# Layer 0's attention: the query side of a tile in three turns, each beside other tiles' steps

## The chip, the cores and the metric

The kernel runs on one core of one Trainium2 chip. The metric is the device time of one launch in microseconds, the median of three runs. A core has an engine for matrix products (TensorE, PE in the profile, which writes its results to eight PSUM banks), two for elementwise work that can read PSUM (VectorE, DVE; ScalarE, ACT), a third for elementwise work and indirect transfers (GpSimd, POOL), and SyncE (SP), which issues most transfers.

## The reference

Four layers work on 1250 nodes with 512 features. Each adds a graph layer and a mixer to x, then a mixture of experts. The mixer of layer 0 is a small network of two blocks, each an attention and a perceptron. Its attention is linear, with 8 heads of 64 features and 256 random features per head:

```python
y = layernorm(x, ln1_g[i], ln1_b[i])
q, k, v = ...                                     # y @ Wq + bq and so on, split into heads
qp = softmax_kernel(q, proj[i], True)             # ratio * (exp(dash - diag - max) + 1e-4), 256 per head
kp = softmax_kernel(k, proj[i], False)
d_inv = 1.0 / einsum('bhnm,bhm->bhn', qp, kp.sum(axis=2))
ctx = einsum('bhnm,bhnd->bhmd', kp, v)
o = einsum('bhmd,bhnm,bhn->bhnd', ctx, qp, d_inv)
x = x + o @ Wo[i] + bo[i]
```

The rest of the program (experts, graph layers, the other mixers) is not touched by the change.

## The kernel before

Nodes are worked on in 10 tiles of 125 and in three chunks of 500, 500 and 250 (`CH`). Everything is float32 where this text goes; a float32 product is two PE instructions in the profile, so that four calls show as x8, while a transpose is one.

`l0_attention` (L843) runs twice, for the two blocks. Its first half makes keys and values and from them `cx`, the context: for each head and each half of the 256 features a 128 x 65 block, whose 65th column is the sum of the keys' features. Its second half, which is what changes, goes over the queries:

- Per chunk, four `proj_T` products give `qT`, the transposed queries, and ScalarE squares them into `sq` (L1049). Both have one buffer.
- `features_q` (L991) makes a tile's features. PE forms half the sum of squares per head (`halves,sq`, one bank) and the products with the random directions (`pj,qT`, four banks); DVE takes the maxima of each bank (L1004) and forms the negative bias `nb` (L1008, L1009); ACT takes the exponentials of the four banks into `qf` (L1012), one head at a time.
- `mixed` (L1015) does the rest of a tile. PE turns `qf` so that features lie on partitions, 16 transposes into four banks (L1020), each emptied by DVE with the addition of 1e-4 and the ratio into `qfT` (L1022). Then come the products with `cx`, four heads to a bank; DVE takes the reciprocal of the 65th columns and multiplies (L1033, L1034) into `ov`. PE turns `ov` (four transposes, L184, one bank), and `copy` empties that bank into `oT`: it takes DVE (L141) and ACT (L143) by turns, over the whole program. At last `oT` times `wo` (`w,oT` in the profile) is added by DVE to the residual (L261).

`mixed` runs one tile behind `features_q`: in each turn of the loop the features of tile t come first, then everything that is left of tile t-1. `aside`, called once a turn, adds edges to the graph in the first block and does nothing in the second.

Which engine an instruction runs on is written in the text. In what order an engine gets its instructions is set by a planner in the tile layer: it goes by the order of the text, and takes a later instruction where an earlier one isn't ready by its own costs. So the statistics of the next layer norm (`BATCH_NORM_STATS`, L191), which the text has behind the attention, stand in DVE's order within it, one after each tile's addition. PSUM banks come from one pool of eight (`bank`, L145). [...]

After the attention, `l0_mlp` normalises all tiles, turns them, and goes through the perceptron in four parts, whose weights use the same three buffers as `wq` and `wo`.

## Time and profile before

| what | value |
|---|---|
| median of 3 runs | 3299.57 us (3297.28 to 3302.95) |
| the profiled execution's own time | 3299.46 us |
| its span, first to last instruction | 3297.7 us |
| mean granted TensorE clock | 0.945 |
| query half, first block | 228 to 420 us: PE busy 172.4 of 193.0 us in 228 to 421 |
| query half, second block | 889 to 1080 us: PE busy 170.8 of 191.0 us |
| DVE, ACT busy in 228 to 421 | 87.8, 41.0 us |

A row of the profile names a line of the kernel, the engine, the operation, and what it writes and reads (out<-in, buffer numbers left out). Busy time counts an engine's own instructions; an idle time stands with the instruction that ended it, and with what that one had waited for. PEclk is the clock that PE was granted, as a share of full speed. Where a product comes from the helper `mm`, its line is L178 whatever calls it, so products are told apart by their tiles.

### The profile page before, as it was taken

The page shows a single profiled execution, that of the slowest core. Times are in us where ns is not written, and L with a number is a line of the kernel's source. Part 1 is how long each engine was busy: PE and PEld are TensorE (multiplying, and loading weights), DVE is VectorE, ACT ScalarE, POOL GpSimd, SP SyncE. Part 2 cuts the span into 40 slices and gives each one's busy share as a digit, 9 for nine tenths or more (in the row PEclk, how much of TensorE's full clock was granted, in tenths as well). Part 3 has the DMA queues.
Part 4 walks back from the last instruction along what each step waited for, and adds up shares of the span by engine and source line. Part 5 has one row for each costly group of instructions (what it writes and reads, how often), then busy time and mean ns, then how long its engine had stood idle before and what let it go on. Part 6 is the DMA issues. An engine that isn't in the chain of part 4 may idle for free. (4 is left out here: it accounts for less than half of the span.)

```text
span 3297.7 us, 31736 instructions
## 1 busy us (share of the span) xinstructions
PE 2947.0 (89%) x11563; PEld 1729.9 (52%) x11563; DVE 1185.3 (36%) x2903; ACT 731.9 (22%) x1511; POOL 677.7 (21%) x497
## 2 busy tenths in 40 slices
PE   7998889989988899989799987999799988779884
PEld 4556645455566454555455445766454547445552
DVE  6834431043344421243541352001334144352433
ACT  2222121122222212122230341221141013320121
POOL 4444444440000210013400011000301002022023
PEclk9999999999899899999899997999899999989987
DMA  7411112110000221217510016776310016530186
GB/s 220 108 14 1 16 17 46 33 30 14 13 1 14 59 69 39 57 37 218 172 47 1 7 32 222 244 241 208 99 39 1 1 53 197 177 103 1 32 291 196
DMA packets 236801, 277.58 MB, mean 84 GB/s; under 512 B 104719, under 2 KB 132735, under 8 KB 236625
## 3 DMA queue, kind: packets, MB, share of 16 engines
q1 hardware_dynamic: 126977, 189.85, 18.0%
q0 software_dynamic: 95968, 60.53, 8.2%
q10 hardware_dynamic: 13680, 24.91, 2.0%
q8 instruction: 104, 1.70, 0.2%
q14 instruction: 72, 0.59, 0.1%
HBM read 229.62 MB, written 45.17 MB: 83 GB/s over the span
## 5 line engine op out<-in xcount | busy, mean ns | idle before, releaser
L178 PE MATMUL ps<-xnT,w 128*128 128x500 f32 (+1 forms) x1584 | 571.9, 517 | 4.4 <-PEq L761 2.3
L178 PE MATMUL ps<-w,hT 128*125 128x512 f32 (+1 forms) x1232 | 540.4, 592 | 0.6 <-ACT hT L1199 0.6
L178 PEld LDWEIGHTS ps<-xnT,w 128*128 128x128 f32 x1584 | 299.9, 191 | 265.9 <-issue 251.2
L683 POOL DMA_INDIRECT adj<-count,cell x160 | 320.4, 2002 | 362.1 <-DMA adj<-count,cell 337.7
L178 PEld LDWEIGHTS ps<-w,hT 128*125 128x125 f32 (+1 forms) x1232 | 230.0, 189 | 276.8 <-issue 270.4
L178 PE MATMUL ps<-w,xnT 128*125 128x512 f32 x560 | 251.3, 598 | 0.0
L178 PE MATMUL ps<-xgT,w 128*128 128x256 f32 (+1 forms) x1256 | 235.3, 346 | 2.5 <-DVE xgT L510 1.7
L261 DVE TENSOR_TENSOR xn<-ps,xn 125x512 f32<-125x512 f32 x100 | 69.0, 691 | 455.2 <-PE ps L178 455.2
L178 PEld LDWEIGHTS ps<-xgT,w 128*128 128x128 f32 x1256 | 208.3, 194 | 43.7 <-issue 20.1
L468 POOL DMA_INDIRECT xg<-rows,r_idx x95 | 90.4, 952 | 627.6 <-PE ps L509 313.5
L587 ACT ACTIVATE hT<-ps,cols 128x500 f32<-128x500 f32 (+1 forms) x108 | 65.7, 608 | 553.1 <-PE ps L178 553.1
L178 PEld LDWEIGHTS ps<-w,xnT 128*125 128x125 f32 x560 | 103.6, 190 | 119.6 <-issue 118.4
L529 POOL DMA_INDIRECT came<-yd,slots x80 | 98.8, 1235 | 315.9 <-SPq L498 249.9
L510 DVE COPY xgT<-ps 128x512 f32<-128x512 f32 x95 | 62.6, 688 | 251.5 <-PE ps L509 233.9
L178 PE MATMUL ps<-hs,AT 125*125 125x512 bf16 x600 | 131.4, 379 | 3.8 <-PEq L761 3.8
L178 PE MATMUL ps<-AT,n 125*128 125x500 bf16 (+1 forms) x720 | 127.2, 339 | 0.0
L519 DVE TENSOR_TENSOR y<-ps,erow 128x512 f32<-128x512 f32 x71 | 49.1, 692 | 196.1 <-PE ps L178 184.1
L520 ACT ACTIVATE y<-y,r_w 128x512 f32<-128x512 f32 x71 | 51.2, 722 | 273.1 <-DVE y L519 254.6
L178 PEld LDWEIGHTS <-AT 125*125 125x125 bf16 x600 | 81.7, 136 | 55.5 <-issue 9.6
L178 PE MATMUL ps<-w,oT 128*125 128x512 f32 x160 | 92.1, 730 | 15.6 <-ACT oT L143 7.1
L184 PE MATMUL ps<-ident,z 125*128 125x125 f32 x320 | 61.1, 340 | 44.9 <-DVE z L199 25.3
L178 PEld LDWEIGHTS <-n 125*128 125x128 bf16 x720 | 69.9, 97 | 58.1 <-issue 1.1
(414 smaller groups left out, 3683.8 us busy)
## 6 DMA issues: line engine op xcount, KB each, us to landing
w<-in_L_ffn_we_dram SPq DMA_DIRECT2D x56, 1024.0 KB
w<-in_L_ffn_w_dram SPq DMA_DIRECT2D x60, 512.0 KB
yd<-y ACTq DMA_DIRECT2D x95, 256.0 KB
w<-in_L_mix_W_dram SPq DMA_DIRECT2D x16, 1024.0 KB
w<-in_L_ffn_w_dram SPq DMA_DIRECT2D x45, 256.0 KB
rows<-z SPq DMA_DIRECT2D x40, 224.0 KB
keyrow<-keys SPq DMA_DIRECT2D x16, 546.9 KB
erow<-in_L_ffn_b_dram SPq DMA_DIRECT2D x30, 256.0 KB
```

The lines of the kernel that those rows point to most:

```text
L178: nc.tensor.matmul(o, l, r, start=(i == 0), stop=(i == n - 1))
L184: nc.tensor.transpose(ps[:, tok(c)], src[:, fea(c)], ident[:TP, :TP])
L261: nc.vector.tensor_tensor(dst, ps, dst, op=OP.add)
L468: nc.gpsimd.indirect_dma_start(g, None, self.rows, bass.IndirectOffsetOnAxis(ap=self.idx[:, t:t + 1], axis=0))
L510: nc.vector.tensor_copy(xgT[:, :, j * SL:(j + 1) * SL], ps.rearrange("p (c s) -> p c s", c=NC))
L519: nc.vector.tensor_tensor(y, ps, bias, op=OP.add)
L520: nc.scalar.mul(y, y, scale)
L529: nc.gpsimd.indirect_dma_start(y, None, yd, bass.IndirectOffsetOnAxis(ap=slots[n][:, k * NT + t:k * NT + t + 1], axis=0))
L587: nc.scalar.activation(hT[:, f, :cn], ps[:, :cn], act, bias=b1(f))
L683: nc.gpsimd.indirect_dma_start(adj, bass.IndirectOffsetOnAxis(ap=self.cell[:, c:c + 1], axis=0), self.count[:, c:c + 1], None, compute_op= ...
```

## The change

`mixed` is cut in four: `turned_q` makes `qfT`, `attended` makes `ov`, `turned_out` makes `oT`, and `project` adds the product with `wo`. A turn of the loop now turns the features of tile t-1, makes the features of tile t, forms the products of tile t-1 with the context, projects tile t-2, and turns the output of tile t-1. The last two tiles are finished behind the loop. `oT` is always copied by ACT.

```diff
-            def mixed(t, qf):
+            def turned_q(qf):
                 qfT = qp.tile([P, H, 2, TP], F32, tag="qfT", name="qfT", bufs=2)
...
+                return qfT
+
+            def attended(qfT):
                 ov = qp.tile([TP, H, C], F32, tag="ov", name="ov")
...
+                return ov
+
+            def turned_out(ov):
                 oT = qp.tile([P, NC, TP], F32, tag="oT", name="oT", bufs=2)
-                copy(oT, transposed(ov.rearrange("p h c -> p (h c)")))
+                nc.scalar.copy(oT, transposed(ov.rearrange("p h c -> p (h c)")))
+                return oT
+
+            def project(t, oT):
                 ps = bank()
                 mm(ps[:TP, :], [(oT[:, c, :], wo[:, c, :]) for c in range(NC)])
                 add_to(xm[:, t, :], ps[:TP, :])
...
-            before = None
+            before, last = None, None
...
                 for t, o in tiles_of(c0, cn):
+                    if before is not None:
+                        qfT = turned_q(before[1])
                     qf = features_q(qT, sq, slice(o, o + TP))
                     if before is not None:
-                        mixed(*before)
+                        ov = attended(qfT)
+                        if last is not None:
+                            project(*last)
+                        last = before[0], turned_out(ov)
                     aside()
                     before = t, qf
-            mixed(*before)
+            qfT = turned_q(before[1])
+            project(*last)
+            oT = turned_out(attended(qfT))
+            project(before[0], oT)
```

## The prediction

> **What bounds the kernel now.** I read the page's first part, then the waits of TensorE (PE) in the two stretches that the change touches, then PE's timeline tile by tile, then the clock.

> The page says that PE is the bound, 2947 of 3297.7 us:

> ```profile
> PE 2947.0 (89%) x11563; PEld 1729.9 (52%) x11563; DVE 1185.3 (36%) x2903; ACT 731.9 (22%) x1511; POOL 677.7 (21%) x497
> ```

> The query half of layer 0's attention runs twice, from 228 to 420 us and from 889.5 to 1079.6 us. Who PE waits for in 228 to 421 (in total us, times, longest):

> ```profile
> PE ps L1020 <- DVE qfT L1022: 5.8, 8, 0.8
> PE ps L184 <- DVE ov L1034: 5.2, 10, 0.5
> PE ps L178 <- ACT oT L143: 3.5, 5, 0.7
> PE ps L178 <- DVE oT L141: 3.5, 4, 0.9
> ```

> Three waits per tile, each for the engine that empties PE's last product. PE's timeline shows what they cost (start, length, work, count, idle before):

> ```profile
> 273.53 3.70 PE L178 MATMUL ps<-w,oT 128*125 128x512 f32 x8 [0.67 <-ACT oT L143]
> 277.07 0.93 PE L178 MATMUL ps<-halves,sq 128*125 128x2 f32 x8
> 277.93 2.10 PE L178 MATMUL ps<-pj,qT 64*125 64x256 f32 x16
> 279.95 1.50 PE L1020 MATMUL ps<-ident,qf 125*128 125x125 f32 x12
> 282.28 0.65 PE L1020 MATMUL ps<-ident,qf 125*128 125x125 f32 x4 [0.83 <-DVE qfT L1022]
> 282.77 3.61 PE L178 MATMUL ps<-cx,qfT 128*125 128x65 f32 x32
> 286.21 0.38 PE L184 MATMUL ps<-ident,ov 125*128 125x125 f32 x2
> 287.11 0.43 PE L184 MATMUL ps<-ident,ov 125*128 125x125 f32 x2 [0.52 <-DVE ov L1034]
> 288.40 5.37 PE L178 MATMUL ps<-w,oT 128*125 128x512 f32 x8 [0.86 <-DVE oT L141]
> 293.61 13.58 PE L178 MATMUL ps<-xnT,w 128*128 128x500 f32 x32
> ...
> 409.16 1.87 PE L1020 MATMUL ps<-ident,qf 125*128 125x125 f32 x16
> 410.87 3.61 PE L178 MATMUL ps<-cx,qfT 128*125 128x65 f32 x32
> ```

> I count from start to start, since lengths contain the drain of the last product. Without waits: features F 277.07 to 279.95, 2.88 us; turning the features T (16 transposes, the row at 409.16) 1.71; products with the context A 3.44; turning the output O, 4 such transposes, 0.43; projection R 273.53 to 277.07, 3.54. Sum 12.00 us. The tile from 262.40 to 277.07 (projection to projection) took 14.67. So a tile loses 2.67 us, more than the 2.2 us of listed waits, because at each wait the pipeline drains too.

> The projection at 288.40 takes 5.37 us, the one at 273.53 3.70: same work. The windows say why (us; PE busy, instructions; granted clock):

> ```profile
> 254.40:257.80 3.40, 2.07 (x14) 1.00 0.13 1
> 257.80:261.20 3.40, 3.40 (x6) 0.50 0.12 1
> ...
> 264.60:268.00 3.40, 2.57 (x23) 1.00 0.09 5
> 268.00:271.40 3.40, 3.40 (x34) 1.00 0.05 0
> 264.60:268.00 3.40, 1.89 (x16) 1.00 0.09 5
> ```

> After a window of 3.4 us in which PE was busy 2.07 us, the next one ran at half clock. The last row counts the transposes alone. Cut into such windows, stretch one holds six half-clock windows (at 257.8, 288.5, 332.9, 350.0, 387.5, 404.6), each after one with 60 to 64% busy, and stretch two five (933.7, 978.0, 995.1, 1025.8, 1063.4). Each costs 5.37 - 3.70 = 1.67 us.

> **The change part by part.** PSUM banks come from a ring of 8 in text order, and in this trace PE takes the steps in text order even while it waits, so I take the new text as PE's new order: T(t-1), F(t), A(t-1), R(t-2), O(t-1).

> No arithmetic is added or taken away: the same matmuls, evictions, exponentials, no DMA, no queue passed over. What moves is what lies between a product and its reader:

> 1. T to A: the four evictions of qfT take 2.42 us on DVE (one group in the trace). They now have F's 2.88 us beside them. From T's start (0), the first bank is full at about 0.5, the last eviction ends by 3.0, and A begins at 1.71 + 2.88 = 4.6. Margin 1.6 us; 0.9 if one BATCH_NORM_STATS (0.69), which the planner puts into DVE's pauses here, stands ahead. The wait goes.
> 2. A to O: reciprocal and division (0.18 + 0.42 us) have R of an older tile, 3.54 us, beside them. The wait goes.
> 3. O to R: the copy of oT (0.57 on ACT) has a whole turn beside it. The wait goes. All copies are now ACT's: five more per stretch, 0.58 us each, in an engine that does 3.6 of 12 us; DVE loses five of 0.68. Without that cover it would be the present 0.7 us.
> 4. New wait: T(t) follows F(t) by A + R + O = 7.4 us; today another F and all of the previous tile lie between. Behind F come the last reduction (0.7), nb twice (0.3) and eight exponentials (3.02): done at about 4.6 + 4.1 = 8.7 on the tile's clock, T(t) at 12.0. Margin 3.3 us; behind that T all of PE would queue. Only in the first tile, which has no A, R, O before its T, does it bite: F(0) ends at 244.6, reductions at 246.0, exponentials from 246.4 to 249.5, T(0) ends at 250.0, F(1) at 252.9; A(0) begins at 252.9 instead of 251.6, 1.3 us late. O(0) has no R ahead and waits about 0.9 as now.
> 5. Banks: T and F together ask for 9 of 8; the ninth needs the first bank of T, emptied at about 1.2, and is asked for at 4.1. Free.
> 6. DVE: 2.6 + 2.5 + 0.8 + 0.7 + 0.7 + 0.4 + 0.6 = 8.3 us per tile (its groups from 262.40 to 277.07), of 12.0. It isn't the bound. What aside adds for the graph DVE has done by 152 us (L677), before stretch one.

> Sum, stretch one: O(0) ends and T(1) begins at about 257.7. Eight turns of 12.00 = 96.0; the projections of q for chunks two and three, 13.4 + 6.75; hence 373.9. Tail: T 1.71, R 3.54, A 3.44, O with both its waits 2.06, R 3.70 = 14.45. End 388.3, today 420.07: 31.8 us less. Stretch two has the same offsets (A(0) at 912.99, now 914.3); 135.4 us later it ends at 1049.7 instead of 1079.63: 29.9 less. Together 61.7; of this 11 x 1.67 = 18.4 is clock and 43.3 order.

> **The clock rule.** In the trace, full windows are followed by full clock. [...] No gap here is over 0.93 us and the clock falls all the same, so the row decides: part of a window idle is enough. [...] The new order puts O and T side by side, 2.14 us of transposes, then 0.86 us of tiny products; if they counted as idle, the clock would fall in many turns. The window at 264.6 was such a one: 1.89 us of transposes, 0.68 of other work, the rest idle, and the clock stayed at 1.00. The window at 254.4 had 0.81 of transposes, 1.26 of other work, and fell. So I count transposes as busy and take the clock as won, except for one window per stretch at the slow first tile or at the tail: 2 x 1.7 = 3.4 us given back.

> 61.7 - 3.4 = 58.3. The profiled execution took 3299.46 us (span 3297.7 and 1.8 around it), 0.1 below the median: **3241 us**.

> Nothing downstream holds this back: the only chain that runs by its own time, POOL's indirect additions to adj, ends at 749 us, and its first reader starts at 1080, about 1020 after the change. The weights for the perceptron are asked for when wq and wo come free (376.35 and 420.10), which move along.

> **The rivals.**
> - Clock not won. For: [...] outcomes near 60 to 65% busy go both ways (at 363.6, 60% busy, it didn't fall). Against: the window at 264.6. 3299.5 - 43.3 = 3256.
> - Half of the waits stay, because the planner orders DVE otherwise than the text: about 3270. For: today it sets nb between the evictions of qfT, where the text has it ahead of them. Against: T's banks are now full before F's.
> - Slower: DVE's order keeps the four reductions of F(t), nb and a BATCH_NORM_STATS ahead of the evictions of qfT. Then the last reduction ends at 5.4, and the evictions end at 5.4 + 0.3 + 0.7 + 2.4 = 8.8 instead of 3.0; A waits 4.2 us. It decides from 2.67 + 18.4/20 = 3.6 us per tile on. Here: (4.2 - 2.67) x 18 turns = +28, and a half-clock window in each turn instead of every other, + 0.75 x 18 = 13: 3340. Against: the bank ring lets F's ninth bank in only after an eviction, so at most part of it can happen.
> - It doesn't do what it says: the planner returns to the old order on PE, 3299. Against: PE has kept to the text in all 20 tiles.

> **How the numbers follow.** Likeliest 0.75 (3241, own range 3233 to 3250: two runs of before lie 5.7 us apart[...]); clock not won 0.12; half 0.06; slower 0.04; no effect 0.03. The range 3232 to 3262 takes in the first two. A change of 0.2%, 6.6 us, is about what a measurement tells from none: faster 0.93, same 0.03, slower 0.04.

> **What would show it.** PE's waits in the two stretches fall from 19.7 us each to about 5; all but the last projection of each stretch take about 3.7; the stretches last about 160 us; PE busy falls by the clock's 15 to 18 us. Wrong would be: rows of PE waiting for qf at L1012 in every turn (point 4), for qfT before A (point 1), or windows of 0.50 after windows full of transposes.

## The result and the profile after

The changed kernel takes 3261.98 us (median of 4, 3259.36 to 3276.86) beside 3301.26 for the kernel before: a ratio of 0.9887, 95% interval 0.9861 to 0.9913. Run again later it took 3260.24 us, ratio 0.9878 (0.9859 to 0.9897). It is faster, by 1.1 to 1.2% where 1.8% was forecast. 3299.57 x 0.9887 is 3262.3, at the upper edge of the range and just outside.

PE's row on the page after:

```profile
PE 2941.7 (90%) x11563; PEld 1740.8 (53%) x11563; DVE 1183.8 (36%) x2893; ACT 737.5 (23%) x1521; POOL 678.6 (21%) x497
```

PE's waits in the first stretch (in total us, times, longest), 228 to 395 us:

```profile
PE ps L1021 <- ACT qf L1012: 2.3, 1, 2.3
PE ps L178 <- ACT oT L1044: 0.7, 1, 0.7
PE ps L184 <- DVE ov L1038: 0.5, 1, 0.5
```

The three waits per tile are gone; one of each of the last two is left, in the last tile, and there is one new one, for the exponentials of the first tile. A turn in the middle of the stretch, in PE's timeline:

```profile
276.87 1.87 PE L1021 MATMUL ps<-ident,qf 125*128 125x125 f32 x16
278.58 0.93 PE L178 MATMUL ps<-halves,sq 128*125 128x2 f32 x8
279.44 2.10 PE L178 MATMUL ps<-pj,qT 64*125 64x256 f32 x16
281.47 3.71 PE L178 MATMUL ps<-cx,qfT 128*125 128x65 f32 x32
285.01 3.65 PE L178 MATMUL ps<-w,oT 128*125 128x512 f32 x8
288.50 0.59 PE L184 MATMUL ps<-ident,ov 125*128 125x125 f32 x4
```

From 276.87 to the next step at 288.92 are 12.05 us, with no idle time. So the new order does what was forecast, turn after turn. The two stretches by themselves (us; PE busy, instructions; granted clock), before and then after:

```profile
228.10:420.10 192.00, 172.25 (x938) 0.95 0.12 7
889.50:1079.60 190.10, 170.38 (x938) 0.96 0.02 6
```

```profile
230.90:395.80 164.90, 161.28 (x938) 0.97 0.13 9
865.30:1040.10 174.80, 171.20 (x938) 0.91 0.02 7
```

They are 27.1 and 15.3 us shorter, 42.4 together; the working of the prediction ends at 160.2 for each. The same work takes 10 us more of PE in the second stretch than in the first, at a clock of 0.91. The place is the second stretch's start:

```profile
880.77 1.14 PE L178 MATMUL ps<-pj,qT 64*125 64x256 f32 x8
884.25 2.65 PE L1021 MATMUL ps<-ident,qf 125*128 125x125 f32 x12 [2.34 <-ACT qf L1012]
886.69 1.68 PE L178 MATMUL ps<-halves,sq 128*125 128x2 f32 x8
...
894.18 6.98 PE L178 MATMUL ps<-cx,qfT 128*125 128x65 f32 x32
...
911.78 3.95 PE L178 MATMUL ps<-cx,qfT 128*125 128x65 f32 x32
915.57 3.65 PE L178 MATMUL ps<-w,oT 128*125 128x512 f32 x8
```

The products with the context take 6.98 us here and 3.71 in the turn shown above. In the clock records of this case's ten traces the granted clock is 1.00 or 0.50, and all its changes lie a whole number of 3.413 us apart; the shortest spell at 0.50 lasts 3.413 us. So I cut the time into windows of that length, at the places where the clock changes:

```profile
878.20:881.60 3.40, 3.40 (x26) 1.00 0.00 0
881.60:885.00 3.40, 1.06 (x9) 1.00 0.00 0
885.10:888.50 3.40, 3.40 (x17) 0.50 0.00 0
888.50:891.90 3.40, 3.40 (x12) 0.50 0.02 5
...
908.90:912.30 3.40, 3.40 (x15) 0.50 0.00 0
912.40:915.80 3.40, 3.40 (x32) 1.00 0.00 0
```

The wait of 2.34 us falls into one window; the next eight run at half clock, although PE is busy in all of each. In the first stretch it is three windows, from 250.1. The second execution of this kernel has three and eight again.

**A measure that fits.** Busy time doesn't tell these windows apart: PE is busy 3.40 us in the window at 874.8, which full clock follows, and in the one at 885.1, which half clock follows. The columns that PE streams do. For every window I summed, from these traces' own records of products and transposes, the columns of each instruction times the share that its contracted rows are of 128, the most that an instruction here contracts. bf16 columns count half: from start to start a 512-wide bf16 instruction takes 0.216 us in the trace of before (60 of them from 1378.53 to 1391.50), a float32 one 0.443 (3.54 us for the eight of a projection). So an instruction of a 512-wide product counts 512 where it contracts all 128 rows, and one of the features' products, 256 wide with 64 rows, counts 128. At full clock the windows that 500-wide products over 128 rows filled held about 4070 such columns (4071 in the one at 1336.4 of before). The ten profiles of this case (before, after and all experiments below) have 9500 windows. Where a window held under 1440 columns, the next one ran at half clock in 1030 of 1030 cases; where it held over 1600, in 0 of 8392; in between, in 54 of 78. It is the same whether the window itself ran at full or at half clock: in the traces of before and after, with the columns shared out by start times, half clock followed 56 of 56 windows at full clock and 150 of 150 at half clock that held under 1440, and 0 of 1624 and 0 of 59 that held over 1600. Other sums separated the windows worse: with the best single mark 21 of the 9500 lie on the wrong side of it, but 76 if the rows are left out, and 208 if the transposes are. The window at 881.6 holds about 590; the following ones, at half clock, 990, 1460, 1350, 1070, 1390, 1310, 1190 and, at last, 1500. The windows with the 65-wide products with the context, the sums of squares with two columns and the 64-row products of the features held 990 to 1460 here at half clock, and the first turns have no 512-wide projection. The clock came back after the window that held 1500; in the first stretch the three held about 1270, 1210 and 1490, and it came back after the third.

This is a fit to this case's ten profiles, with marks taken from all of them, until something is predicted with it; the run "The same work, behind the fall" below does that. What inside the chip sets the clock, these traces don't show. The theories that the experiments tell apart:
- **Clock theory:** the first tile's wait empties a window, the clock falls, and the mix of the first turns holds it down.
- **Order theory:** the late start costs by itself, the clock is a bystander.
- **Mix theory:** transposes side by side and the missing projection pull the clock down without any wait.

### The profile page after: what moved, and what is told of

It is laid out like the page before. It is cut to its first block, busy times and chain, and to the rows that moved or that the text cites. A ratio compares the mean times of both kernels' runs of the same rounds, so it can differ in the third digit from the quotient of the medians.

```text
span 3262.5 us, 31754 instructions
## 1 busy us (share of the span) xinstructions
PE 2941.7 (90%) x11563; PEld 1740.8 (53%) x11563; DVE 1183.8 (36%) x2893; ACT 737.5 (23%) x1521; POOL 678.6 (21%) x497
## 5 line engine op out<-in xcount | busy, mean ns | idle before, releaser
L178 PE MATMUL ps<-xnT,w 128*128 128x500 f32 (+1 forms) x1584 | 577.3, 520 | 4.3 <-PEq L761 2.2
L178 PE MATMUL ps<-w,hT 128*125 128x512 f32 (+1 forms) x1232 | 540.9, 593 | 0.6 <-ACT hT L1218 0.6
L178 PEld LDWEIGHTS ps<-xnT,w 128*128 128x128 f32 x1584 | 301.6, 192 | 267.3 <-issue 252.8
L178 PEld LDWEIGHTS ps<-w,hT 128*125 128x125 f32 (+1 forms) x1232 | 230.4, 189 | 277.1 <-issue 270.9
L178 PE MATMUL ps<-w,xnT 128*125 128x512 f32 x560 | 253.0, 602 | 0.0
L178 PE MATMUL ps<-xgT,w 128*128 128x256 f32 (+1 forms) x1256 | 234.8, 345 | 2.5 <-DVE xgT L510 2.5
L178 PEld LDWEIGHTS ps<-xgT,w 128*128 128x128 f32 x1256 | 208.0, 193 | 43.6 <-issue 18.9
L178 PEld LDWEIGHTS ps<-w,xnT 128*125 128x125 f32 x560 | 104.3, 192 | 120.6 <-issue 120.0
L178 PE MATMUL ps<-hs,AT 125*125 125x512 bf16 x600 | 134.2, 385 | 3.9 <-PEq L761 3.9
L178 PE MATMUL ps<-AT,n 125*128 125x500 bf16 (+1 forms) x720 | 127.2, 339 | 0.0
L178 PEld LDWEIGHTS <-AT 125*125 125x125 bf16 x600 | 82.9, 139 | 57.2 <-issue 12.3
L184 PE MATMUL ps<-ident,z 125*128 125x125 f32 x320 | 61.7, 343 | 44.0 <-DVE z L199 23.4
L178 PEld LDWEIGHTS <-n 125*128 125x128 bf16 x720 | 70.0, 97 | 58.0 <-issue 1.1
L178 PE MATMUL ps<-mix,qT 128*125 128x512 f32 x160 | 76.9, 625 | 14.3 <-ACT qT L1263 14.3
```

Of the source, the lines that this page charges most:

```text
L178: nc.tensor.matmul(o, l, r, start=(i == 0), stop=(i == n - 1))
L184: nc.tensor.transpose(ps[:, tok(c)], src[:, fea(c)], ident[:TP, :TP])
```

## The experiments

**The changed kernel again.**

> The changed kernel once more, for another execution's clock. Clock theory: the first tile of each stretch turns its features right behind making them, PE waits 2.3 us for the exponentials, the clock window that holds this wait streams too little, the next ones run at half clock, and the first turns, which have no projection, can't lift it again. So the wait of 2.3 us is there again in both stretches, a run of half-clock windows follows it, of another length than 3 and 8[...]; about 3262 us. Order theory (the late start itself costs, the clock is a bystander): the same places, 3262 us.

3260.24 us, 3257.36 to 3273.99. The stretches take 165.2 and 174.8 us, the waits for the exponentials are 2.7 and about 2.3. That the runs of half-clock windows would differ was a miss: three and eight again. The windows lay within about 1 us of where they lay in the first profile.

**Features first in the first turn alone.**

```diff
-                    if before is not None:
+                    if last is not None:
                         qfT = turned_q(before[1])
                     qf = features_q(qT, sq, slice(o, o + TP))
+                    if before is not None and last is None:
+                        qfT = turned_q(before[1])
```

> Only the first turn has its features ahead of the turning, as the kernel before has them. Clock theory: no wait of 2.3 us, clock 1.00 through both starts; from a stretch's first projection of q to its first products with the context 23.5 us (29.0 and 28.9 in the changed kernel's profile), from there to the second ones 9.4 (9.6 and 17.6): 19 us less in all, about 3243 us. Order theory: only the waits and the shifted steps go, 2 x 2.5 us: 3257. A third theory, that transposes side by side and the missing projection pull the clock down without any wait: half-clock windows in the first turns stay, 3255 to 3260 us.

3241.63 us (3238.92 to 3242.93), ratio 0.981 (0.9797 to 0.9824). Both stretches, and the windows at the first one's start:

```profile
231.70:390.40 158.70, 156.36 (x938) 1.00 0.13 9
860.30:1019.00 158.70, 156.35 (x938) 1.00 0.02 7
245.70:249.10 3.40, 3.40 (x28) 1.00 0.09 5
249.10:252.50 3.40, 2.47 (x16) 1.00 0.12 1
252.50:255.90 3.40, 3.34 (x27) 1.00 0.12 1
```

There is no half-clock window in either stretch, and each takes 158.70 us. The 22.3 us that the stretches lose against the changed kernel are the 19 of the clock theory and some. The order theory (3257) and the mix theory (3255 to 3260) miss by 13 us and more. A wait of 0.93 us for the exponentials is left in this start as in the kernel before, and its window, with PE busy 2.47 us, holds about 1700 columns: the next window ran at 1.00.

**More work, in the wait.**

```diff
+                    if before is not None and last is None:
+                        mm(bank()[:TP, :], [(yT[:, c, tok(0)], wq[:, c, :]) for c in range(NC)])
                     if before is not None:
                         qfT = turned_q(before[1])
```

> The changed kernel with one more product of 512 columns (four calls, 3.54 us, its result is not used) in the first turn, where PE waits for the exponentials. More work for PE, the wait filled by it. Clock theory: the windows there stream enough, clock 1.00 through both starts; the products with the context begin about 25.5 us into a stretch and the second ones 9.4 later, 15 us less than the changed kernel in all: about 3247 us. Order theory: the product costs what it doesn't cover, 2 x 0.7 us, nothing is won: 3263 us. Third theory (mix of work): half-clock windows stay, 3260 us or more.

3243.31 us (3235.36 to 3246.76), ratio 0.9814 (0.98 to 0.9828): 17 us less than the changed kernel, with eight more PE instructions in each stretch. The start of the first stretch, and both stretches:

```profile
247.66 1.14 PE L178 MATMUL ps<-pj,qT 64*125 64x256 f32 x8
248.72 3.70 PE L178 MATMUL ps<-w,xnT 128*125 128x512 f32 x8
252.26 1.92 PE L1021 MATMUL ps<-ident,qf 125*128 125x125 f32 x16
...
256.91 3.71 PE L178 MATMUL ps<-cx,qfT 128*125 128x65 f32 x32
```

```profile
232.20:392.60 160.40, 159.16 (x946) 1.00 0.13 9
860.00:1020.40 160.40, 159.16 (x946) 1.00 0.02 7
```

The text's order of the steps is that of the changed kernel, and the tile still starts late; only the window is full. The clock stays at 1.00, and the products with the context begin 24.7 us into the stretch instead of 28.9 to 29.0. That decides between clock and order: by order alone this run would have been slower than the changed kernel.

**The same work, behind the fall.** The unused product takes the place of the missing projection instead, and the wait stays:

```diff
                         if last is not None:
                             project(*last)
+                        else:
+                            mm(bank()[:TP, :], [(yT[:, c, tok(0)], wq[:, c, :]) for c in range(NC)])
```

> The changed kernel with one unused product of 512 columns in the first turn in place of the projection that is missing there, behind the products with the context; the wait of 2.3 us ahead stays. Clock theory: the fall stays where it is, but the second stretch gets back to full clock after the window full of that product: about 6 half-clock windows instead of 8; the first stretch, back before it, keeps 3. The product costs 3.5 us in each stretch and wins 3.4 in the second: about 3265 us. If what was won in the other filled kernel came from anything but the windows' streaming at the wait, 8 windows stay and it costs 7 to 10 us: 3270.

3266.99 us (3262.16 to 3269.87), ratio 0.9884 (0.9865 to 0.9903). In the second stretch:

```profile
893.30:896.70 3.40, 1.06 (x8) 1.00 0.00 0
896.70:900.10 3.40, 3.40 (x18) 0.50 0.02 5
...
913.80:917.20 3.40, 3.40 (x6) 0.50 0.00 0
917.20:920.60 3.40, 3.40 (x25) 1.00 0.00 0
```

Six half-clock windows instead of eight, as forecast from the sum of columns: the window at 913.8, full of the 512-wide product at half clock, holds about 2100, and the next one is at full clock. In the first stretch there were also six, where three were forecast: a miss. There the third half-clock window held about 1360 columns, where that of the changed kernel held about 1490 and was the last. Each stretch takes 172.8 us. So in the second the product won about what it cost (174.8 in the changed kernel, with one half-clock window more in its tail), and in the first it cost 7.9 us. The time, 3267 us, lies between the two that were expected, 3265 and 3270, and doesn't decide between them; the count of windows in the second stretch does. The filler won 17 us in the wait and nothing behind the fall, so its place made them.

**Features first in every turn**, which undoes the first of the three moves:

```diff
-                    if before is not None:
-                        qfT = turned_q(before[1])
                     qf = features_q(qT, sq, slice(o, o + TP))
+                    if before is not None:
+                        qfT = turned_q(before[1])
```

> Features ahead of the turning in every turn; the deferred projection stays. This undoes the first of the three moves alone. The wait of the fourth bank of turned features for an eviction (0.83 us, 1.05 from start to start) comes back in 18 turns, 19 us; the wait in the first tile goes with what hangs on it. Clock theory: the two cancel, about 3262 us, with clock 1.00 at both starts. Order theory: 3262 + 19 - 5 = 3276 us.

3259.02 us (3255.97 to 3262.54), ratio 0.9866 (0.9851 to 0.9882). PE's waits in the first stretch, and both stretches:

```profile
PE ps L1021 <- DVE qfT L1023: 5.3, 8, 0.8
PE ps L178 <- ACT qf L1012: 1.1, 1, 1.1
```

```profile
229.90:398.20 168.30, 160.61 (x938) 0.99 0.13 8
868.00:1036.30 168.30, 160.70 (x938) 0.99 0.02 7
```

Against the run with features first in the first turn alone, each stretch is 9.6 us longer, 19.2 in all: the first move's worth is the 19 forecast from 1.05 us per turn. In the changed kernel it is paid back in full by the first tile. So of the three moves as written, the first wins nothing.

**The output ahead of the older projection:**

```diff
-                        if last is not None:
-                            project(*last)
-                        last = before[0], turned_out(ov)
+                        oT = turned_out(ov)
+                        if last is not None:
+                            project(*last)
+                        last = before[0], oT
```

> The output is turned ahead of the older tile's projection, so that the wait for ov has lost its written cover; the planner sets one of the projection's four calls (0.88 us) between the two halves of that turning, which covers the 0.6 us of DVE nearly. So by the waits alone about the same as the changed kernel, 3260 to 3266 us; if the cover has to be the whole projection, 18 x 0.9 us more, 3277. Clock theory: starts unchanged, runs of 3 and 8 half-clock windows.

3265.56 us (3255.93 to 3270.16), ratio 0.9879 (0.9853 to 0.9905), not told apart from the changed kernel. The planner cut the steps up:

```profile
315.50 0.38 PE L184 MATMUL ps<-ident,ov 125*128 125x125 f32 x2
315.71 1.02 PE L178 MATMUL ps<-w,oT 128*125 128x512 f32 x2
316.58 0.38 PE L184 MATMUL ps<-ident,ov 125*128 125x125 f32 x2
316.79 2.74 PE L178 MATMUL ps<-w,oT 128*125 128x512 f32 x6
```

One call of the projection, 0.87 us from start to start, was enough cover here: no wait for ov is left in the first stretch. Half-clock windows were eight at both starts here, where three and eight were forecast: a miss for the first, and that it comes from where the windows fell is the author's estimate.

**The projection in its own tile's turn:**

```diff
-                        if last is not None:
-                            project(*last)
-                        last = before[0], turned_out(ov)
+                        project(before[0], turned_out(ov))
...
-            project(*last)
```

> The projection belongs to its own tile's turn again, behind the turning of the output; the turning of the features stays ahead of the next features. This keeps the first move alone. PE waits for ov and for oT again, 1.6 us in 18 turns, 29 us, and the window that holds both waits and the narrow products streams little, so that half-clock windows come back in about every other turn, 15 us: 3262 + 44 = 3306 us; against the kernel before the first move wins 18 x 1.05 = 19 us and its start loses as much: 3300. Without a clock effect of these waits: 3291.

3320.56 us (3315.03 to 3323.11), ratio 1.0054 (1.0036 to 1.0072): slower than before, and 15 us above the higher estimate. A turn on PE, and what ACT did meanwhile:

```profile
341.05 0.43 PE L184 MATMUL ps<-ident,ov 125*128 125x125 f32 x2 [0.52 <-DVE ov L1038]
343.16 2.75 PE L178 MATMUL ps<-w,oT 128*125 128x512 f32 x3 [1.68 <-ACT oT L1044]
```

```profile
339.62 3.03 ACT L1012 ACTIVATE qf<-ps,nb 125x256 f32<-125x256 f32 x8 [11.20 <-DVE mv L192]
342.49 0.63 ACT L1044 COPY oT<-ps 128x500 f32<-128x500 f32 x1
```

The copy of oT now stands behind eight exponentials, which wait for DVE until 339.62; the wait for it grows from 0.8 to as much as 2.0 us. Over both stretches these waits add up to 28.1 us, beside 13.9 in the kernel before. That was not in the estimate, and it is about the 15 us by which the run exceeded the estimate. The stretches hold seven and eleven half-clock windows here, three and nine in the changed kernel: six more, where about nine were expected. So the deferred projection carries the change: it covers the wait for ov, the wait for oT and this queue.

**The copies on both engines again** (`copy(` for `nc.scalar.copy(`):

> The copies of oT go to DVE and ACT by turns again, nothing else. A whole turn lies between copy and reader, and DVE has 8 of 12 us to do: the same as the changed kernel within 0.2%, 3262 us. If DVE's order were near its limit, PE rows waiting for qfT would appear, + 0.7 us in 10 turns: 3269.

3267.11 us (3248.71 to 3273.41), ratio 0.9881 (0.9841 to 0.9921). The stretches take 165.4 and 174.8 us, those of the changed kernel within half a microsecond, and no wait is new. Which engine copies made no difference here, where a turn lies between copy and reader.

## Why the prediction was right or wrong

- **Points 1 to 3, the three covers:** right. 12.05 us per turn against 12.00, no idle time, the listed waits down from 19.7 to 3.5 us per stretch (forecast about 5), all projections at full clock but the second stretch's last. In the rows of before a step's length exceeds the time from start to start by 0.16 to 0.17 us (1.87 beside 1.71, 3.61 beside 3.44, 3.70 beside 3.54), and three times that, an estimate, is the 0.5 us between 2.67 and the 2.2 of listed waits.
- **Points 5 and 6, banks and DVE:** right; no row of PE waits for either in a turn.
- **Point 4, the new wait:** right in its place and its own size. The exponentials of the first tile were to end at 249.5, 21.4 us into the stretch; they ended 21.5 us into it. What lies behind them was forecast too short. The products with the context were to begin 1.3 us late; they began 5.4 to 5.5 us later than before, counted from the stretch's start, in both stretches (29.0 and 28.9 us against 23.5). In the second stretch the next tile's were late by 8 us more. The exponentials and the first products with the context, in the kernel after (start 230.9) and, last row, before (start 228.1):

```profile
249.30 3.02 ACT L1012 ACTIVATE qf<-ps,nb 125x256 f32<-125x256 f32 x8 [3.38 <-DVE nb L1009]
259.82 3.96 PE L178 MATMUL ps<-cx,qfT 128*125 128x65 f32 x32
251.60 3.61 PE L178 MATMUL ps<-cx,qfT 128*125 128x65 f32 x32
```

  From the end of the exponentials to these products 3.4 us were forecast and 7.5 measured, and the three half-clock windows from 250.1 cover all of it.
- **The term that failed:** "except for one window per stretch at the slow first tile or at the tail: 2 x 1.7 = 3.4 us given back". It measured 164.9 + 174.8 - 2 x 160.2 = 19.3 us: 10.2 us at half clock in the first stretch and 30.7 in the second, of which about half is lost (1.67 us of 3.4 by the two projections of before). The difference, 15.9 us, is the whole gap between the forecast gain in the stretches, 58.3, and the measured 42.4; with features first in the first turn the gap is closed (158.7 us per stretch), and its 3241.6 us is about what had been forecast for the change itself. The step behind the term was to take a half-clock window as single, because full windows were seen to be followed by full clock. In the trace of before they are single in these stretches, and each holds a projection of 512 columns; the new first turns have none, and the sum of columns could have been made from the rows at hand. PE's busy time, which was to fall by 15 to 18 us, fell by 5.3: it fell by 11.0 in the first stretch, rose by 0.8 in the second, for the same reason, and rose by 4.9 elsewhere.
- **The clock rule:** I read the rows as "part of a window idle is enough". That was the wrong measure: windows with PE busy 3.40 of 3.40 us kept half clock, seven of the eight in the second stretch. That full windows are followed by full clock did not hold throughout in the trace of before either. Three of its 719 full windows were followed by half clock, one of them with products one column wide in 2.2 of its 3.4 us:

```profile
1343.30:1346.70 3.40, 3.40 (x25) 1.00 0.00 0
1346.70:1350.10 3.40, 3.40 (x5) 0.50 0.00 0
```

  That window held about 1440 columns. Taking the transposes as busy was borne out for these float32 ones: counted by their columns they fit with the rest, 21 windows of 9500 on the wrong side of the best mark beside 208 without them. The weight of 0.12 on a clock not won was the author's estimate.
- **The clock's gain in the turns:** right; of the 11 half-clock windows of before none came back in the turns behind the starts; one, at 1035.2, lies in the last tile.
- **Rivals:** none held. The time is nearest to that of the clock not won (3256), but by another mechanism: the clock was won in the turns and lost at the two starts.

Downstream, the profiled execution gained 35.2 us of span where the stretches gained 42.4, and the second execution gained 42.0. So the first missed the forecast by 23 us, 15.9 in the stretches and 7 elsewhere, and the second lost nothing elsewhere. Outside the stretches the two executions have 100 and 95 half-clock windows, and that of before 95; five more at 1.7 us would be 8 us (an estimate). That is argued from the counts and not tested.

## What to carry to other kernels

When a loop is turned so that each step lies beside another tile's, work through its first turns by themselves: a step that was moved ahead of its cover has no cover there, and a wait that is small against the loop can cost several times its length: here 2.34 us of it, with eight half-clock windows behind, in a stretch of 174.8 us beside 158.70 with features first in the first turn. Where PE is the bound, sum for the windows between clock changes what PE streams, columns times contracted rows, beside its busy time; in these traces the sum told which windows half clock followed, and busy time didn't. A wide product set into the wait won 17 us here, though its result is thrown away, but reordering one turn won as much without it. Of a change in several moves, run each alone: here one move carried it and another won 19 us and lost them in its first turn.
